# ACT's instructions in program order over 35 groups of a feed-forward stage

## The chip, the cores and the metric

The kernel runs on one core of a Trainium2 chip. The metric is the device time of one execution in microseconds (us), the median of three runs. A core has five engines that run beside each other, each through its own list of instructions in a fixed order: PE (TensorE, matmuls, with a separate weight load PEld), DVE (VectorE), ACT (ScalarE), POOL (GpSimd) and SP (SyncE, which here only issues DMAs). An instruction whose data are not ready holds up everything behind it on its engine.

## The reference

```python
x = x + 0.5 * ffn(layernorm(x), w1, b1, w2, b2)      # 256 -> 1024, relu, -> 256
u = layernorm(x)
K = 2 * real(einsum('hn,hnl->hl', Ct, exp(dtA * l)))  # 256 channels, N = 64 states
y = irfft(rfft(u, 2L) * rfft(K, 2L))[:, :L]           # causal convolution, L = 2048
x = x + (layernorm(u + y + u * D) * ln_w + ln_b)
x = x + 0.5 * ffn(layernorm(x), w1, b1, w2, b2)
```

x has the shape 8 x 2048 x 256 in float32. All matmuls with the weights are made in three parts (a high and a low half of each operand), so that they keep nearly full float32 accuracy.

## The kernel before

The tokens are worked on in 64 **groups** of 256. Stage a is the first feed-forward half step, stage b the second; between them the convolution is computed by chunks of 128 positions, with tables of powers of the states. This case is about stage a, and about the tables, which are built while it runs.

`sublayer` (L876) writes stage a out in **steps**, 8 to a group; step 3 of group 24 is called slot 24.3. One step takes one 128-wide chunk of the 1024 hidden columns:

- `up` (L851, matmul L857): 6 matmuls on PE into one of 4 PSUM banks `ph`.
- ACT: relu of that bank, the high half of the hidden tile `hx` (L946).
- DVE: max minus the high half, the low half of `hx` (L947, recorded at L116).
- `down` (matmul L867): 6 matmuls of the step that lies LAG = 3 steps behind, into `po`. So a relu must be done before the `down` three steps later.

Beside that each group has on ACT two norms `xn` and two norms `u` (L726), the copy `xh` of the transposed input (L799), one square root (L686) and two DMA issues (store of x1 L1030, load of `xa` L1012); on POOL one `add_bias` (L773), which waits for ACT's `xn`. PE turns the input by four transposes up to group 43 (`pt_a`, L790); from group 44 on DMAs do it (`DMA_A = 44`).

The **background** is a generator, `chain(matrices(), early())`. `fill()` (L902) lets it make a step whenever a virtual time, 1.32 for each step of the stage, has passed the sum of its paces. So a planes' batch is due each 9.1 units (10.3 from the 18th on), and its instructions are traced between those of the stage. `matrices()` builds a table P in 32 batches, here called planes 0 to 31. Each goes through three parts, one pass of the loop (L648) apart:

- `make(bt)` (L590): six products on POOL, L599, L601, L603, L605, L607 and L609, into a buffer `p_of(bt)`. There are four buffers in each half of the 32, so `make(bt)` can write only when the batch four before it has been stored. L609 is the last.
- `spread(bt)` (L612): two ACT copies (L618) of the low and high 16 bits into the tile `planes`, then one transposing DMA on SP's queue (L620) from `planes` to `turned`, and a DMA of the table itself (L625). There is one `planes` and one `turned`, so the copies of a batch wait until the DMA of the batch before has read them.
- `transpose(bt)` (L628): the back copies out of `turned`, one on DVE and one on ACT (both L635), and the store of the turned table (L637).

```python
yield
yield
for w in range(2):
    tc.keep_in_program_order(A_.copy(planes[:, w], pu[:, w]))
    yield
tc.keep_in_program_order(nc.sync.dma_start(
    out=turned..., in_=planes..., transpose=True))
```

In the trace both tiles are named `planes` (the DMA is planes<-planes), and P's buffers are parts of the large tile `u`. Beside the three parts, `lags()` adds small products on POOL (L535, L537, L541), matmuls `pk` on PE (L549) and four DMA issues on POOL (L569).

What sets the order: a scheduler takes the traced instructions and puts those of each engine into the order in which its own timeline finds them ready. Two things bind it: `keep_in_program_order`, which pins an instruction against the other pinned ones of its engine, and `tc.manual_schedule(engines=...)`, inside of which the named engines follow the traced order as it is. Before, the latter is used only for ACT and DVE in the steps ahead of t = 0 of a stage (L920 to L927, closed at t == 0). So in steady state ACT's relus and norms are free to move past the copies of `planes`, and the copies past them.

Of the kernel before, what the change touches and what calls it, by code (L numbers as in the profile page):

```python
# [43 lines left out]
def macaron_s4d_kernel(  # L44
# [35 lines left out]
    XL = 8  # L80
    LAGS_BEHIND = 3
    PIN = 1
    PINF = "a1", "a2"
    MB = 1
    PINT = 1
# [23 lines left out]
    def bank(tag, name):  # L109
        return ps.tile([P, 512], F32, name=name, tag=tag, bufs=BANKS[tag])  # L110

    def slot(tag, shape, name, dtype=F32):
        return work.tile(shape, dtype, name=name, tag=tag, bufs=BUFS[tag])

    def stt(o, a, s, b, op0, op1):
        return V.scalar_tensor_tensor(out=o, in0=a, scalar=s, in1=b, op0=op0, op1=op1)  # L116
# [554 lines left out]
    def stats(srcs, name, pin=False, mv=None):  # L671
        st = stat.tile([P, NTB, 6], F32, name=f"st_{name}", tag="st")
        mv = moments(NTB, name) if mv is None else mv
        for i, src in enumerate(srcs):
            ins = V.bn_stats(st[:, i, :], src)
            if pin:
                tc.keep_in_program_order(ins)
        for i in range(NTB):
            V.bn_aggr(mv[:, i, :], st[:, i, :])
        return mv  # L680
# [64 lines left out]
    def halves(xt):  # L745
        return [xt[:, i, :] for i in range(NTB)]

    def ffn_in(xt, name, on_act=NTB, by_dma=False, joint=None, into=None):
# [7 lines left out]
        else:  # L756
            mv = stats(halves(xt), f"f{name}", name in PINF)
            yield
# [92 lines left out]
    def up(wt, xT, ph, fc):  # L851
        xh, xl = xT
        fs = slice(fc * P, (fc + 1) * P)
        n = 0
        for dc in range(NDC):
            for wp, xp in ((1, xh), (0, xl), (0, xh)):
                nc.tensor.matmul(  # L857
                    ph, wt[wp][:, dc, fs], xp[dc] if type(xp) is list else xp[:, dc, :], start=(n == 0), stop=(n == 3 * NDC - 1)
                )
                n += 1  # L860

    def down(wt, hs, po, fc):
        hh, hl = hs
        for i in range(NTB):
            tsl = slice(i * P, (i + 1) * P)
            for n, (hp, wp) in enumerate(((hl, 0), (hh, 1), (hh, 0))):
                nc.tensor.matmul(  # L867
                    po[:, i, :],
                    hp[:, tsl],
                    wt[wp][:, fc, :],  # L870
                    start=(fc == 0 and i == 0 and n == 0),
                    stop=(fc == NFC - 1 and n == 2),
                    skip_group_check=True,
                )

    def sublayer(w1t, w2t, pre, post, lead, tag, first=(), background=(), due=(), at=(), wide=None):  # L876

        xT, po, running = {}, {}, {}
        background = iter(background)
        due = dict(due)
        at = dict(at)
        now = [0.0, 0.0]
        last = {}

        def step():  # L890
            while spawned:
                key, what = spawned.pop(0)
                running["later", key] = what
            for key in list(running):
                try:
                    next(running[key])
                except StopIteration as e:
                    del running[key]
                    if key[0] == "pre":
                        xT[key[1]] = e.value  # L900

        def fill(until=None):  # L902
            while until or now[1] <= now[0]:
                pace = next(background, "end")
                if isinstance(pace, str):
                    due.pop(pace, None)
                    if pace == "end":
                        now[1] = math.inf
                    if pace in (until, "end"):
                        return  # L910
                else:
                    now[1] += pace

        W0, W1 = (wide.first, wide.end) if wide else (NG, NG)
        starts_at = {}
        for g in range(NG):
            sooner = wide.sooner(g) if wide else 0
            starts_at.setdefault(g * SLOTS - lead - sooner, []).append(g)

        ordered = ExitStack()  # L920
        if first or tag == "b" and MB:
            ordered.enter_context(
                tc.manual_schedule(engines={mybir.EngineType.Activation, mybir.EngineType.DVE})
            )
        for t in range(-lead, NG * SLOTS + LAG + 1):
            if t == 0:
                ordered.close()  # L927
            g, k, f = t // SLOTS, t % SLOTS // 2, t % 2
            if W0 <= g < W1:
                g0, fc = g // 2 * 2, (t - g // 2 * 2 * SLOTS) // 2  # L930
                if f == 0:
                    hx = wide.hidden()
                    for i in range(2):
                        pend[g0 + i, fc] = [h[:, i * TOK : (i + 1) * TOK] for h in hx]
                    ph = bank("h", f"ph_{tag}{g0}_{fc}")
                    up(w1t, wide.input(g0), ph, fc)
                    last[A_] = A_.activation(hx[0], ph, AF.Relu)  # L937
                    last[V] = stt(hx[1], ph, 0.0, hx[0].bitcast(F32), ALU.max, ALU.subtract)
            elif t >= 0 and g < NG:
                fc = 2 * k + f  # L940
                hx = slot("hx", [P, 2, TOK], f"hx_{tag}{g}_{fc}", F32R)
                hh, hl = pend[g, fc] = hx[:, 0], hx[:, 1]
                ph = bank("h", f"ph_{tag}{g}_{fc}")[:, 0:TOK]
                up(w1t, xT[g], ph, fc)

                last[A_] = A_.activation(hh, ph, AF.Relu)  # L946
                last[V] = stt(hl, ph, 0.0, hh.bitcast(F32), ALU.max, ALU.subtract)  # L947
            tb = t - LAG
            tw = t - WLAG
            if W0 * SLOTS <= tw < W1 * SLOTS:  # L950
                g0 = tw // (2 * SLOTS) * 2
                fc, i = divmod(tw - g0 * SLOTS, 2)
                if fc == 0:
                    po[g0 + i] = wide.result(f"po_{tag}{g0 + i}").rearrange("p (i m) -> p i m", i=NTB)
                down(w2t, pend.pop((g0 + i, fc)), po[g0 + i], fc)
                if fc == NFC - 1:
                    running["post", g0 + i] = post(g0 + i, po.pop(g0 + i))
            if 0 <= tb < NG * SLOTS and not W0 * SLOTS <= tb < W1 * SLOTS:
                gb, fc = tb // SLOTS, tb % SLOTS
                if tb % SLOTS == 0:  # L960
                    po[gb] = bank("o", f"po_{tag}{gb}").rearrange("p (i m) -> p i m", i=NTB)
                down(w2t, pend.pop((gb, fc)), po[gb], fc)
                for mark in [m for m, d in due.items() if d == gb]:
                    fill(mark)
                if tb % SLOTS == SLOTS - 1:
                    running["post", gb] = post(gb, po.pop(gb))
            for n in starts_at.get(t, ()):
                running["pre", n] = pre(n)
            if t == -lead:
                running["first"] = iter(first)  # L970
            step()
            if t >= 0:
                now[0] += 1.32
                with ExitStack() as behind:
                    for ins in last.values():
                        behind.enter_context(tc.issue_after(ins.ins))
                    fill()
            if t in at:
                at[t]()
        while running:  # L980
            step()
        fill("end")
# [285 lines left out]
    def begin():  # L1268
        for _ in range(sizes[1] // PB):
            next(head)  # L1270

    sublayer(
        w1t, w2t, pre_a, post_a, 19, "a", load_weights(), chain(matrices(), early()),
        {"half": NG // 2, "tables": NG * 3 // 4},
# [123 lines left out]
    def pre_b(g):  # L1398
# [8 lines left out]
        uc = [uo[:, i // CQ, :, i % CQ] for i in range(P - 1 - i0, P - 1 - i0 - NTB, -1)]  # L1407
        mv = stats(uc, f"r{g}", PIN & 2)
        yield
# [9 lines left out]
        for i in range(NTB):  # L1419
            xb = xt[:, i, :].rearrange("p (b h) -> p b h", h=BCH)  # L1420
            ins = stt(xb, uc[i], rs[:, i : i + 1], xb, ALU.mult, ALU.add)
            if PIN & 1:
                tc.keep_in_program_order(ins)
# [4 lines left out]
    def post_b(g, po):  # L1428
# [7 lines left out]
        )  # L1436

    sublayer(
        [wb1[:, i] for i in range(2)], [wb2[:, i] for i in range(2)], pre_b, post_b, 17, "b",
        wide=wide,  # L1440
# [33 lines left out]
```

## Time and profile before

| | us |
|---|---|
| runs | 1746.32, 1751.17, 1751.95; median 1751.17 |
| profiled execution | 1747.17 |
| its span, first to last instruction | 1745.3 |
| mean granted clock of PE in it | 0.994 of full speed |
| groups 14 to 48 of stage a | 183.9 to 618.1 |
| one group in a calm part: groups up to 43, from 44 | 11.94, 11.52 |
| first and last copy of planes (L618) | 221.1, 575.0 |

The profile is of one execution; its times count from the first instruction. A row of a timeline has start, length, engine, line, operation, output<-inputs with shapes and, in brackets, the idle time of the engine just ahead and what ended it. Rows of one kind that follow each other are put together (x6). A row of waits has what waited, for what, and the total, the number and the longest in us. A row of windows has the stretch, its length, and the busy time and number of instructions of each engine in it.

### The profile page before, as it was taken

Reading aid. Unit: us, or ns where it says so; the run is one execution under the profiler, and the core shown is the slowest. Engines: PE = TensorE matmul, PEld = TensorE weight load, DVE = VectorE, ACT = ScalarE, POOL = GpSimd, SP = SyncE. Lnnn points to the kernel's source line nnn. Section 1 sums busy time; section 2 is a strip of 40 time slices with the busy share of each in tenths; the row PEclk is TensorE's granted clock in tenths of the full one; section 3 lists DMA queues with packets and bytes.
Section 4 is the critical chain, followed back from the end, with each engine's and each line's share of the span. In section 5 each row is a group of like instructions: output and inputs, shape, how many; then the busy total and the mean of one; then the engine's idle time right before and its main releaser. Section 6 shows DMA issues by size and latency. Waiting matters only on the chain.

```text
span 1745.3 us, 38327 instructions
## 1 busy us (share of the span) xinstructions
PE 1713.1 (98%) x14263; PEld 1638.1 (94%) x14263; DVE 1368.3 (78%) x4591; ACT 968.4 (55%) x2040; POOL 586.3 (34%) x550
## 2 busy tenths in 40 slices
PE   9999999999999999999999899999999999999998
PEld 7999999989999999999999799999999999999998
DVE  6998776677777767766999788889888788788754
ACT  4555477677778755544555445555455455445533
POOL 1117989886776105111000132231222222222200
PEclk9999999999999999999999989999999999999999
DMA  5111166577666532236888912332223323222211
GB/s 191 47 40 53 49 178 164 160 199 205 188 167 190 134 85 68 73 91 194 263 259 260 292 49 72 70 90 56 67 73 73 73 67 79 73 67 73 63 48 37
DMA packets 276849, 204.24 MB, mean 117 GB/s; under 512 B 162740, under 2 KB 235188, under 8 KB 276150
## 3 DMA queue, kind: packets, MB, share of 16 engines
q1 hardware_dynamic: 249232, 168.08, 36.2%
q10 hardware_dynamic: 26502, 32.52, 5.9%
q8 instruction: 112, 1.84, 0.4%
q0 software_dynamic: 928, 1.19, 0.3%
q14 instruction: 75, 0.61, 0.1%
HBM read 91.89 MB, written 71.57 MB: 94 GB/s over the span
## 4 chain that ended last, share of the span: by engine, by line
PE 80%; DVE 12%; DMA 4%; issue 1%; ACT 1%; SPq 0%; POOL 0%; ACTq 0%; DVEq 0%
PE po_b L867 21%; PE ph_b L857 20%; PE po_a L867 19%; PE ph_a L857 18%; DVE e L1160 2%; DMA planes<-planes 2%; DVE te L1161 2%; DVE xsB L1163 1%; DVE xsA L1163 1%; PE pt_a L790 1%; DVE xsA L1162 1%; DVE xsB L1162 1%; DMA xa<-in_L_attn_x_dram 1%; DMA wb<-w_dram 1%; PE pv L1130 1%
## 5 line engine op out<-in xcount | busy, mean ns | idle before, releaser
L867 PE MATMUL po_a<-wa,hx_a 128*128 128x256 f32 x3072 | 454.7, 285 | 6.8 <-DVE hx_a L116 6.6
L857 PE MATMUL ph_a<-xh_a,wa 128*128 128x256 f32 x2048 | 456.4, 287 | 1.2 <-ACT xh_a L799 0.7
L867 PEld LDWEIGHTS po_a<-wa,hx_a 128*128 128x128 f32 x3072 | 405.3, 192 | 9.5 <-DVE hx_a L116 8.0
L857 PEld LDWEIGHTS ph_a<-xh_a,wa 128*128 128x128 f32 x2048 | 355.3, 193 | 4.3 <-ACT wa L194 1.5
L946 ACT ACTIVATE hx_a<-ph_a 128x256 fp32r<-128x256 f32 x512 | 193.8, 388 | 229.5 <-PE ph_a L857 207.4
L116 DVE SCALAR_TENSOR_TENSOR hx_a<-ph_a,hx_a 128x256 fp32r<-128x256 f32 x512 | 209.0, 414 | 121.8 <-ACT hx_a L946 119.8
L867 PEld LDWEIGHTS po_b<-wb,hb 128*128 128x128 f32 x2208 | 288.1, 191 | 14.4
L867 PE MATMUL po_b<-wb,hb 128*128 128x256 f32 x2208 | 292.6, 282 | 0.0
L857 PE MATMUL ph_a<-xl_a,wa 128*128 128x256 f32 x1024 | 290.3, 285 | 0.0
L857 PE MATMUL ph_b<-xh_b,wb 128*128 128x256 f32 (+1 forms) x928 | 249.8, 327 | 0.7 <-ACT xh_b L799 0.7
L937 ACT ACTIVATE hb<-ph_b 128x512 fp32r<-128x512 f32 x184 | 109.2, 594 | 162.1 <-PE ph_b L857 161.2
L857 PEld LDWEIGHTS ph_a<-xl_a,wa 128*128 128x128 f32 x1024 | 197.4, 193 | 0.6 <-DVE xl_a L801 0.4
L116 DVE SCALAR_TENSOR_TENSOR hb<-ph_b,hb 128x512 fp32r<-128x512 f32 x184 | 124.9, 679 | 83.3 <-ACT hb L937 81.0
L773 POOL TENSOR_TENSOR xa<-xa,hb 128x512 f32<-128x512 f32 x64 | 85.1, 1330 | 286.9 <-ACT xn L726 245.9
L857 PEld LDWEIGHTS ph_b<-xh_b,wb 128*128 128x128 f32 x928 | 167.3, 193 | 12.8 <-ACT xh_b L799 1.1
L857 PE MATMUL ph_b<-xl_b,wb 128*128 128x256 f32 (+1 forms) x464 | 151.1, 327 | 0.0
L857 PE MATMUL ph_b<-even,wb 128*128 128x512 f32 x576 | 149.0, 393 | 0.0
L867 PE MATMUL po_b<-wb,hx_b 128*128 128x256 f32 x864 | 126.5, 285 | 3.9 <-DVE hx_b L116 3.9
L867 PEld LDWEIGHTS po_b<-wb,hx_b 128*128 128x128 f32 x864 | 114.2, 193 | 4.8 <-DVE hx_b L116 4.5
L857 PEld LDWEIGHTS ph_b<-even,wb 128*128 128x128 f32 x576 | 102.4, 189 | 16.9
L773 POOL TENSOR_TENSOR u<-u,hb 128x512 f32<-128x512 f32 x32 | 46.4, 1449 | 177.0 <-ACT xn L726 144.6
L946 ACT ACTIVATE hx_b<-ph_b 128x256 fp32r<-128x256 f32 x144 | 54.0, 381 | 73.0 <-PE ph_b L857 67.9
(292 smaller groups left out, 3028.4 us busy)
## 6 DMA issues: line engine op xcount, KB each, us to landing
o<-u SPq DMA_DIRECT2D x32, 512.0 KB, 4.0
pt<-u SPq DMA_DIRECT2D x32, 512.0 KB, 4.0
tz<-kpad SPq DMA_DIRECT2D x64, 256.0 KB, 4.5
x_dram<-xa ACTq DMA_DIRECT2D x62, 256.0 KB, 2.1
xa<-in_L_attn_x_dram ACTq DMA_DIRECT2D x61, 256.0 KB, 3.0
pt<-pt SPq DMA_DIRECT2D x60, 256.0 KB, 3.7
ot<-o SPq DMA_DIRECT2D x48, 256.0 KB, 4.1
u<-x_dram SPq DMA_DIRECT2D x32, 256.0 KB, 2.8
```

The source lines that it names most:

```text
L116: return V.scalar_tensor_tensor(out=o, in0=a, scalar=s, in1=b, op0=op0, op1=op1)
L773: return G_.tensor_add(xt, xt, hb2.unsqueeze(1).to_broadcast([P, NTB, H]))
L790: nc.tensor.transpose(pt[:, dc * TOK + i * P : dc * TOK + (i + 1) * P], xn[:, i, dc * P : (dc + 1) * P], ident,)
L857: nc.tensor.matmul(ph, wt[wp][:, dc, fs], xp[dc] if type(xp) is list else xp[:, dc, :], start=(n == 0), stop=(n == 3 * NDC - 1))
L867: nc.tensor.matmul(po[:, i, :], hp[:, tsl], wt[wp][:, fc, :], start=(fc == 0 and i == 0 and n == 0), stop=(fc == NFC - 1 and n == 2), skip ...
L937: last[A_] = A_.activation(hx[0], ph, AF.Relu)
L946: last[A_] = A_.activation(hh, ph, AF.Relu)
L1130: ins = nc.tensor.matmul(pv[ri][c * N : (c + 1) * N, l, j0 * B : j1 * B], pts[c][:, l, ri * N : (ri + 1) * N], some(j0, j1)[:, :, BCH * bt ...
L1160: E.tensor_mul(t1, xv[:, :, :, j, :], wr_b)
L1161: E.tensor_mul(t2, xv[:, ::-1, :, j, :], wi_b)
L1162: E.tensor_add(xv[:, :, :, j + 1, :], xv[:, :, :, j + 1, :], t1)
L1163: E.tensor_add(xv[:, :, :, j + 1, :], xv[:, :, :, j + 1, :], t2)
```

## The change

One constant, and a branch in the loop of `sublayer`: in stage a, at step 112 (group 14) a `manual_schedule` for ACT alone is opened, at step 392 (group 49) it is closed. What is traced for ACT in between stands on ACT in the order of the program. No instruction is added, removed or changed in shape. Since the scheduler follows the moved ACT instructions with the other engines, POOL's, DVE's and SP's orders differ in places too. Lines behind the first insertion are one higher after, lines behind the second nine.

```diff
@@ -80,6 +80,7 @@
     LAGS_BEHIND = 3
     PIN = 1
+    ACT_ORDER = 14 * 8, 49 * 8
     PINF = "a1", "a2"
@@ -925,6 +926,14 @@
         for t in range(-lead, NG * SLOTS + LAG + 1):
             if t == 0:
                 ordered.close()
+
+            if tag == "a" and t in ACT_ORDER:
+                if t == ACT_ORDER[0]:
+                    ordered.enter_context(
+                        tc.manual_schedule(engines={mybir.EngineType.Activation})
+                    )
+                else:
+                    ordered.close()
             g, k, f = t // SLOTS, t % SLOTS // 2, t % 2
```

## The prediction

> **What bounds it now.** First the page: where the span goes, and whether one engine fills it.
>
> ```profile
> span 1745.3 us, 38327 instructions
> PE 1713.1 (98%) x14263; PEld 1638.1 (94%) x14263; DVE 1368.3 (78%) x4591; ACT 968.4 (55%) x2040; POOL 586.3 (34%) x550
> ```
>
> PE (TensorE) is busy for 98%, so the change, which touches no matmul, can win only where PE stands still. Next, the stretches of stage a between the 14th and the 49th group (busy us and counts of PE, its weight load, DVE, ACT, POOL; granted clock; DMA share; GB/s):
>
> ```profile
> core 0: us, PE busy (x) PEld busy (x) DVE busy (x) ACT busy (x) POOL busy (x), PEclk, DMA share, GB/s
> ...
> 337.00:345.00 8.00, 6.15 (x39) 5.95 (x38) 5.76 (x18) 6.27 (x12) 1.33 (x1) 0.79 0.61 171
> 345.00:395.00 50.00, 45.86 (x379) 45.22 (x378) 34.86 (x130) 37.22 (x70) 42.52 (x39) 1.00 0.72 192
> ```
>
> PE lacks 1.85 us of 8 and 4.14 us of 50 here, and in the first stretch its clock is down. The stretches ahead and behind are full within 0.2 us each up to 545 us. What ACT waits for there (waits of ACT, 184 to 420 us), then the chain itself, ACT's and PE's timelines:
>
> ```profile
> ACT planes L618 <- DMA planes<-planes: 11.6, 9, 3.7
> ...
> ACT planes L618 <- POOL u L609: 1.3, 1, 1.3
> ```
> ```profile
> 332.09 0.38 ACT L946 ACTIVATE hx_a<-ph_a 128x256 fp32r<-128x256 f32 x1 [1.31 <-PE ph_a L857]
> 336.13 1.99 ACT L618 COPY planes<-u 128x1024 uint16<-128x1024 uint16 x2 [3.65 <-DMA planes<-planes]
> 338.03 1.32 ACT L635 COPY u<-planes 128x1024 uint16<-128x1024 uint16 x1
> 339.23 0.64 ACT L946 ACTIVATE hx_a<-ph_a 128x256 fp32r<-128x256 f32 x2
> ```
> ```profile
> 340.10 1.65 PE L867 MATMUL po_a<-wa,hx_a 128*128 128x256 f32 x6 [1.85 <-DVE hx_a L116]
> ```
> ```profile
> 392.93 0.98 PE L867 MATMUL po_a<-wa,hx_a 128*128 128x256 f32 x6 [2.86 <-DVE hx_a L116]
> ```
>
> Three copies stand back to back, with no relu between them. The first waits 3.65 us for the transposing DMA, and the next relu starts at 339.23, although its `up` matmuls ended at 333.94: 5.29 us late. `down` needs that relu, and PE stands. **Slack of a relu:** in a calm slot `down` starts 4.16 us after the end of `up`; relu start to end of DVE's second half takes 0.85 (slot 24.5: 317.39 to 318.24). So a relu may be 4.16 − 0.85 = 3.3 us late for nothing.
>
> **What PE loses between groups 14 and 49 before.** 0.97 in small gaps up to group 25, 1.85 at 338, 1.5 from half clock (the clock row 340.14 to 343.55; 16 matmuls at 0.21 instead of 0.12 us), 0.92 at 353.6, 0.36 at 356.9, 2.86 at 389.8, and 1.4 in small gaps: 9.9 us by group 33. That is all the change could give.
>
> **What the change moves.** By the instruction orders of both programs nothing is added or removed; planes 18 to 31 stand within one slot of where they stood, planes 0 to 17 do not. Written group.slot of the relu ahead: plane 6 copies from 22.5 to 21.6 and 21.7; plane 8 from 25.3 to 23.4 and 23.5; plane 9 from 25.6 to 24.3 and 24.4; plane 10 from 26.2 to 25.1 and 25.3; plane 12 from 28.5 to 26.7 and 27.0. From plane 6 on copies stand 7 slots apart, about 7 × 1.49 = 10.4 us. The back copies (L635, ACT and DVE) stand 6 to 10 slots after them, and SP's transposing DMAs and table stores follow.
>
> *Spreading.* Between two copies now stands at least one relu, except where the back copy follows the second. A bunch of 1.05 + 1.05 + 1.37 = 3.5 us shrinks to 1.05, or 2.4, under the 3.3 of slack. If the data were there, the 1.85, 0.92, 0.36 and 2.86 would go, with the 1.5 of clock: a gain of 7.5.
>
> *Coming early.* A copy can't start until POOL has made its plane (last product L609). Rows of POOL between planes 0 and 9:
>
> ```profile
> 218.80:329.30 110.50, 110.38 (x924) 109.65 (x922) 81.03 (x285) 78.09 (x147) 100.50 (x101) 1.00 0.59 166
> ```
> ```profile
> 328.01 1.29 POOL L609 TENSOR_TENSOR u<-u 128x512 f32<-128x512 f32 x1
> ```
> ```profile
> 314.07 0.38 ACT L946 ACTIVATE hx_a<-ph_a 128x256 fp32r<-128x256 f32 x1 [0.41 <-PE ph_a L857]
> ```
>
> Plane 9 is finished at 329.3; of the 110.5 us since plane 0, POOL was busy 100.5, so no order makes it much earlier: what stands ahead of it on POOL is the same set in both programs. Before, its copy came at 336.1 and the plane was ready. After, it comes behind relu 24.3, which ran at 314.07. ACT then stands, and every later relu, norm, xh copy, and both DMA issues of ACT's queue stand behind it. POOL's 10.0 us of idle were these:
>
> ```profile
> POOL u L599 <- DVE hx_a L116: 3.5, 1, 3.5
> POOL u L599 <- DVE mv_j L679: 2.0, 1, 2.0
> POOL xa L773 <- ACT xn L726: 1.4, 1, 1.4
> POOL u L541 <- PE pk L549: 0.9, 1, 0.9
> ```
>
> The 3.5 waits for a table's store to free the buffer; that store is no earlier after. 2.2 are gaps between dependent products. The other 4.3 may go or stay. Plane 9: 218.8 + 100.5 + 3.5 + 2.2 = 325.0 without them, 329.3 with all, 321.5 if the 3.5 went too. I take 327, the middle of the likely ends. Then copy 1.05, relu and DVE 0.85: 328.9. `down` of slot 24.4 started at 320.07, on an undisturbed grid (0.97 less) at 319.1. **PE slips 9.8 us** (4.3 at 321.5; 12.1 at 329.3). Plane 6 waits too: POOL, without the idle it can lose, ends it near 286.6, while ACT arrives near 280.4; that is 6.2 late, 2.7 of slip, and contained in the 9.8, since later waits shrink by what PE has slipped. The same holds for plane 8 (308.5 against 302.6).
>
> *Clock.* An idle start gap of 2.1 us before brought 3.4 us of half clock; 2.86 us at 390 brought none. A gap several times as long I price like the first, between 0 and 3.4; I take 2.0.
>
> The Trainium skill, "TensorE: Matmul & The Clock Gate", section "Part 1: The HAM clock gate (the "warmup" mystery)", says that the clock halves after an idle window of about 3.4 us and returns after as long a busy one. The 2.1 us row disagrees, the 2.86 us row agrees. By the page before should have lost nothing to the clock, and the one long gap after would cost about 1.7 us; so it speaks against the change, as the sum does.
>
> *After plane 9.* POOL's next chains are 5.0 us each: planes 10 and 11 near 332 and 337, ahead of their copies (25.1 is about 322 + 9.8 + 2 = 334). Plane 10's copies also wait for plane 9's transposing DMA: 0 to 2.4, I take 0.5. Later the loop copy, copy, DMA, next copy took 7.7 (336.1 to 343.8) to 9.1 us (343.8 to 352.9) before; with a relu between the copies about 0.5 more, 8.2 to 9.6 against 10.4: it fits, with little room. I take 1.0.
>
> **Sum.** After: 9.8 + 2.0 + 0.5 + 1.0 = 13.3. Before: 9.9. Net 3.4 us slower. The profiled execution took 1747.17 (span 1745.3 and 1.87 around it), so it would be 1750.6; the median of the three runs is 4.0 above that execution, and the same difference on it gives **1754.6**.
>
> **Rivals.** *Slower than can be missed, the loop of the planes:* the window from 345 to 420 us has the busiest DMA of the stage (share 0.72 and 0.79). If the transposing DMA then needs its longest, 7.5 us to landing instead of the median 4.7, the loop is 8.2 + 2.8 = 11.0 to 12.4, over 10.4, and each of planes 10 to 17 slips 0.6 to 2 us. It decides once the loop passes 10.4 us and the 3.3 us of slack are used up: 8 × 1.3 = 10, less 3.3, so 6.7 more: net +10, near 1761. For it: ACT already waited 11.6 us for that DMA. Against: behind plane 18 the same spaced order ran without loss.
>
> *Faster:* the 9.9 go and POOL's waits fit into the slack. That needs plane 9 by 313.1 + 3.3 + 1 = about 317 us; POOL would have to drop 100.5 to 98 us of work. Halfway (321.5, 4.3 lost, no clock drop) gives 9.9 − 4.3 = 5.6 less, near 1745.5; with all gone 1741. Against: POOL's 91% in that stretch.
>
> *It does nothing that matters:* the waits before were for the DMA, not for the order, and return at the same size: 1751.
>
> **Chances.** Forecast (one long wait at plane 9, then calm; net −2 to +7.5) 0.50; loop rival 0.36; faster rival 0.10; nothing 0.04. About 0.3%, 5.2 us, is what a measurement can tell from no change. Faster 0.10; within, 0.44 of the forecast and 0.04: 0.48; slower, 0.36 and 0.06: 0.42. Range 1745 to 1766: from POOL's early end (321.5) to its late one plus the loop (+2.3 + 6.7 + 2).
>
> **What would show it.** Right: PE idle by about 7 to 10 us in all between 285 and 330 us, behind a planes copy whose wait names POOL L609; the clock down right after; the idle at 338 and 390 gone; planes from 18 on unchanged. Loop rival: several waits of planes copies on DMA planes<-planes from 345 to 420 us, each with PE idle. Faster: no wait on L609 over 3.3 us. Wrong altogether: a loss behind 545 us, where no order differs.

## The result and the profile after

| | before | after |
|---|---|---|
| median, us | 1751.56 (1746.32 to 1753.08, 4 runs) | 1766.82 (1765.47 to 1767.19, 4 runs) |
| ratio, 95% interval | | 1.009 (1.0072 to 1.0109) |
| span of the profiled execution | 1745.3 | 1764.9 |

The change makes the kernel 15.3 us slower; 1754.6 was forecast, and the time lies 0.8 us above the range. The spans differ by 19.6, because the profiled execution of before was a fast one of its kind (1747.17 against the median). How it differs can be seen: four runs below keep before's places of the copies up to group 32 (program order from group 33 or 35 on), and at group 33 their traces are 2.6 to 3.3 us behind it, some 1.5 us of that by a stretch of half clock near 395 us.

The page of after, then the windows of after and those of before that the prediction does not show (columns as there):

```profile
span 1764.9 us, 38328 instructions
...
PE 1719.1 (97%) x14263; PEld 1640.1 (93%) x14263; DVE 1370.7 (78%) x4591; ACT 963.2 (55%) x2040; POOL 587.0 (33%) x550
```
```profile
250.00:300.00 50.00, 42.76 (x340) 41.69 (x339) 34.53 (x105) 30.50 (x58) 39.26 (x40) 0.97 0.54 150
300.00:337.00 37.00, 30.37 (x253) 30.17 (x253) 21.38 (x76) 21.97 (x42) 34.42 (x35) 0.95 0.66 171
337.00:345.00 8.00, 8.00 (x57) 8.00 (x58) 6.24 (x26) 5.37 (x12) 7.53 (x7) 0.82 0.85 245
345.00:395.00 50.00, 48.06 (x396) 47.04 (x395) 35.53 (x130) 35.72 (x69) 42.94 (x40) 1.00 0.67 189
420.00:545.00 125.00, 123.33 (x1014) 121.43 (x1013) 86.67 (x332) 87.82 (x172) 77.46 (x66) 1.00 0.57 165
545.00:635.00 90.00, 87.24 (x716) 85.91 (x715) 67.70 (x246) 64.91 (x131) 29.90 (x25) 1.00 0.53 144
```
```profile
250.00:300.00 50.00, 49.94 (x418) 49.56 (x418) 35.87 (x133) 35.55 (x68) 45.98 (x45) 1.00 0.66 180
300.00:337.00 37.00, 36.94 (x309) 36.59 (x308) 25.87 (x91) 22.67 (x45) 35.92 (x37) 1.00 0.50 147
420.00:545.00 125.00, 125.00 (x1050) 125.00 (x1049) 95.54 (x351) 94.26 (x181) 87.70 (x74) 1.00 0.63 177
545.00:620.00 75.00, 74.44 (x620) 74.27 (x620) 57.12 (x205) 57.09 (x114) 18.91 (x17) 1.00 0.57 146
```

PE is now idle 7.2 us between 250 and 300 and 6.6 between 300 and 337, where before had 0.06 each. It is less idle between 345 and 395 (1.9 instead of 4.1), and it lost 1.7 us between 420 and 545, where before had nothing, and 2.8 between 545 and 635, where before had 0.6 up to 620. To see when the lag arises I took the start of each group's first `down` matmul after, less the same before: 1.2 us in group 19, 2.4 at the start of 21, 11.0 in 22, 10.5 at 24.2, 18.2 at 24.6. Then before has its own stalls, and the lag falls: 14.6 in group 26, 12.9 at 33. From there it grows again, mostly by 0.4 to 0.5 a group and by 2.0 in group 42, to 20.4 at group 46. So there are **two losses**, one up to group 25 and one from 33 on. ACT's waits from 184 to 635 us name both:

```profile
ACT xn L727 <- DVE nb_u L120: 36.9, 22, 4.1
...
ACT planes L619 <- POOL u L610: 17.2, 4, 7.0
ACT planes L619 <- DMA planes<-planes: 16.5, 7, 4.3
```

In before, from 184 to 620 us, the same three rows are 8.1 us (9 waits, the longest 1.3), 1.3 (one wait) and 17.6 (16 waits, the longest 3.7). So the waits for DVE's constants and for POOL are new, those for the transposing DMA are not.

**The first loss.** Copies wait for POOL as forecast, but longer. The chain behind plane 6, from DVE's, SP's, POOL's and ACT's timelines of after (a queue's rows are DMA issues):

```profile
278.98 5.25 DVE L636 COPY u<-planes 128x1024 uint16<-128x1024 uint16 x1
```
```profile
284.29 1.93 SPq L621 DMA_TRANSPOSE planes<-planes  x1
286.27 0.99 SPq L638 DMA_DIRECT2D pt<-u  x1
```
```profile
291.21 1.06 POOL L600 TENSOR_TENSOR u<-u 128x512 f32<-128x512 f32 x1 [7.58 <-DMA pt<-u]
```
```profile
294.57 1.04 ACT L619 COPY planes<-u 128x1024 uint16<-128x1024 uint16 x1 [5.58 <-POOL u L610]
```

DVE's back copy of plane 4 takes 5.25 us. Plane 5's transposing DMA must wait for it, as it writes `turned`; the store of plane 4 stands behind that DMA on SP's queue. POOL's first product of plane 8 reuses plane 4's buffer and waits 7.58 us for the store. And plane 6's last product stands *behind* that first product on POOL. So the copy of plane 6, which ACT may no longer put off, waits 5.58 us, with the relus behind it. At plane 9 the same ring closes again: plane 7's store was issued at 325.10, POOL went on at 330.55 (2.03 us of idle, for which the view names no engine).

```profile
335.01 1.04 ACT L619 COPY planes<-u 128x1024 uint16<-128x1024 uint16 x1 [6.96 <-POOL u L610]
```

PE then shows both what the DVE copy did directly (it held up the low halves that stand behind it on DVE) and what plane 9 did:

```profile
285.64 1.65 PE L868 MATMUL po_a<-wa,hx_a 128*128 128x256 f32 x6 [4.42 <-DVE hx_a L117]
```
```profile
336.85 1.65 PE L868 MATMUL po_a<-wa,hx_a 128*128 128x256 f32 x6 [6.12 <-DVE hx_a L117]
```

The granted clock was at half from 285.3 to 288.7 and from 333.1 to 339.9 us.

**The second loss.** Slot 39.0 and 39.1 on ACT, before and then after:

```profile
499.55 0.38 ACT L946 ACTIVATE hx_a<-ph_a 128x256 fp32r<-128x256 f32 x1 [1.06 <-DVE nb_u L119]
499.90 1.09 ACT L726 ACTIVATE xn<-xa,nb_u,t_u 128x255 f32<-128x255 f32 x2
501.05 0.39 ACT L946 ACTIVATE hx_a<-ph_a 128x256 fp32r<-128x256 f32 x1
```
```profile
515.27 0.38 ACT L955 ACTIVATE hx_a<-ph_a 128x256 fp32r<-128x256 f32 x1 [1.12 <-PE ph_a L858]
516.99 1.09 ACT L727 ACTIVATE xn<-xa,nb_u,t_u 128x255 f32<-128x255 f32 x2 [1.33 <-DVE nb_u L120]
517.98 1.03 ACT L619 COPY planes<-u 128x1024 uint16<-128x1024 uint16 x1
518.92 0.37 ACT L955 ACTIVATE hx_a<-ph_a 128x256 fp32r<-128x256 f32 x1
```

The norm xn waits for DVE's constants `nb_u`, a copy stands behind it, and relu 39.1 comes 2.25 us after its matmuls instead of 0.10. Two slots on, relu 39.3 is 4.0 us late, over the 3.3 of slack, and PE loses 0.2 to 0.5 us. ACT's rows from `xh` to that relu, and PE's `down`:

```profile
521.46 0.59 ACT L800 CAST xh_a<-pt_a 128x512 fp32r<-128x512 f32 x1 [1.19 <-PE pt_a L791]
...
522.60 1.08 ACT L619 COPY planes<-u 128x1024 uint16<-128x1024 uint16 x1
...
523.56 0.39 ACT L955 ACTIVATE hx_a<-ph_a 128x256 fp32r<-128x256 f32 x1
```
```profile
524.47 0.98 PE L868 MATMUL po_a<-wa,hx_a 128*128 128x256 f32 x6 [0.18 <-DVE hx_a L117]
```

In DVE's order `nb_u` stands ahead of the low half of slot 39.0 in before, and behind it in after; the scheduler put the next group's statistics (`st_fa`) and that low half ahead of it:

```profile
499.07 0.58 DVE L119 TENSOR_SCALAR nb_u<-mv_j,t_u 128x1 f32<-128x1 f32 x4
499.57 0.42 DVE L675 BATCH_NORM_STATS2 st_fa<-xa 128x6 f32<-128x256 f32 x1
499.97 0.42 DVE L116 SCALAR_TENSOR_TENSOR hx_a<-ph_a,hx_a 128x256 fp32r<-128x256 f32 x1
```
```profile
516.20 0.41 DVE L117 SCALAR_TENSOR_TENSOR hx_a<-ph_a,hx_a 128x256 fp32r<-128x256 f32 x1
516.53 0.17 DVE L709 RECIPROCAL t_u<-q_u 128x4 f32<-128x4 f32 x1
516.74 0.58 DVE L120 TENSOR_SCALAR nb_u<-mv_j,t_u 128x1 f32<-128x1 f32 x4
```

### The profile page after: what moved, and what is told of

Same layout as the page of the kernel before. It is cut to its first block, busy times and chain, and to the rows that moved or that the text cites. A ratio compares the mean times of both kernels' runs of the same rounds, so it can differ in the third digit from the quotient of the medians.

```text
span 1764.9 us, 38328 instructions
## 1 busy us (share of the span) xinstructions
PE 1719.1 (97%) x14263; PEld 1640.1 (93%) x14263; DVE 1370.7 (78%) x4591; ACT 963.2 (55%) x2040; POOL 587.0 (33%) x550
## 4 chain that ended last, share of the span: by engine, by line
PE 72%; DMA 5%; DVE 4%; ACT 3%; issue 1%; POOL 0%; SPq 0%; ACTq 0%; DVEq 0%; POOLq 0%
PE po_b L868 20%; PE ph_b L858 20%; PE po_a L868 12%; PE ph_a L858 11%; PE py L1214 3%; PE pv L1139 3%; PE py L1205 2%; DMA pt<-pt 1%; DMA planes<-planes 1%; DMA xa<-in_L_attn_x_dram 1%; ACT u L727 1%; ACT planes L619 1%; DMA xb<-x_dram 1%; ACT hx_a L955 1%; DVE hx_a L117 0%
## 5 line engine op out<-in xcount | busy, mean ns | idle before, releaser
L858 PEld LDWEIGHTS ph_b<-xl_b,wb 128*128 128x128 f32 x464 | 89.8, 193 | 3.8
```

The costliest lines, as they stand in the source:

```text
L858: nc.tensor.matmul(ph, wt[wp][:, dc, fs], xp[dc] if type(xp) is list else xp[:, dc, :], start=(n == 0), stop=(n == 3 * NDC - 1))
```

## The experiments

Each run is told with its median and that of the kernel before on the same chip. All start from the changed kernel.

| run | us | before | ratio, 95% interval |
|---|---|---|---|
| e1 groups 33 to 48 only | 1762.72 | 1751.71 | 1.0062 (1.0048 to 1.0075) |
| e2 groups 14 to 32 only | 1762.19 | 1751.71 | 1.0054 (1.0040 to 1.0067) |
| e3 groups 25 to 32 only | 1754.86 | 1751.71 | 1.0026 (1.0015 to 1.0036) |
| e4 as e1, DVE too | 1764.42 | 1751.71 | 1.0067 (1.0055 to 1.0080) |
| e5 as e2, pace 10.3 | 1741.99 | 1750.26 | 0.9956 (0.9942 to 0.9970) |
| e6 before, pace 10.3 | 1740.07 | 1750.26 | 0.9944 (0.9925 to 0.9962) |
| e7 as e2, both back copies on ACT | 1778.84 | 1750.26 | 1.0154 (1.0132 to 1.0177) |
| e8 slot 27.4 to group 32 only | 1756.93 | 1750.26 | 1.0040 (1.0025 to 1.0055) |
| e9 groups 35 to 41 only | 1750.73 | 1751.01 | 1.0003 (0.9992 to 1.0014) |
| e10 as e9, DVE too | 1755.68 | 1751.01 | 1.0029 (1.0018 to 1.0039) |
| e11 after, pace 10.3 | 1746.86 | 1751.01 | 0.9980 (0.9969 to 0.9992) |
| e12 as e2, store ahead | 1764.83 | 1751.01 | 1.0082 (1.0066 to 1.0098) |

**e1 and e2: one part of the order at a time.**

```diff
-    ACT_ORDER = 14 * 8, 49 * 8
+    ACT_ORDER = 33 * 8, 49 * 8      # e1
+    ACT_ORDER = 14 * 8, 33 * 8      # e2
```

> ACT in program order only from group 33 to 48; up to there everything stands as before. The lag of the changed kernel's down matmuls grew by 7.5 us between groups 33 and 49, where the planes' copies stand almost where they stood. Theory 1 (two separate losses: up to group 33 the copies that wait for POOL, from 33 on norms xn that wait on ACT for DVE's constants nb_u with relus queued behind them): the late part alone costs 7 to 8 us, about 1759 us against 1751.5. Theory 2 (one loss; the late lag is only an after-effect of the early waits, since the background then runs at other places of the groups): as before, 1751 to 1752.

> ACT in program order only from group 14 to 32. Theory 1 (two separate losses): the lag reached by group 33 stays, 12.9 us, about 1764 us, and the waits of xn for nb_u behind 430 us are gone. Theory 2 (one loss with after-effects): all of the changed kernel's loss, about 1767 us.

Two losses, as theory 1 said, but the sizes only partly: the late part alone costs 11.0 us, the early part alone 10.5, and together 15.3. e2 loses little behind group 33 (its lag behind before's trace goes from 14.0 to 15.7). e1 pays 4.1 us in group 34, which the whole change doesn't: behind the place where the order is opened the copy of plane 20 waits 3.88 us for the transposing DMA of plane 19, and the clock halves at 453.5. Without that, e1's groups 36 to 40 take 12.3 to 12.7 us as in after, against 11.86 to 12.02 before.

**e3 and e8: the order opened behind the late planes.**

```diff
+    ACT_ORDER = 25 * 8, 33 * 8          # e3
+    ACT_ORDER = 27 * 8 + 4, 33 * 8      # e8
```

> ACT in program order only from group 25 to 32, so that planes 0 to 7 are copied where they were before, planes 8 and 9 in one bunch at slot 25.1, and planes 10 to 17 spaced as in the changed kernel. Theory 1 (the early loss comes from copies that ACT must make ahead of POOL's products; the spacing itself gains): no wait for POOL L610 over 3 us, the 7.5 us that before loses at 338, 354 and 390 us go, and the bunch at 25.1 costs 2 to 4: 1746 to 1749 us. Rival (program order is itself what costs, by the norms and the loop of the transposing DMA): no gain, 1751 to 1756 us.

> ACT in program order from slot 27.4 to group 32 only, behind the planes that POOL delivers late. Planes 0 to 11 stand as before, 13 to 17 are spaced. Theory 1 (spacing gains where the data are there): the 2.9 us of idle at 390 us and the half clock that some executions have behind it go: 1747 to 1749 us. Rival (opening the program order costs by itself, as the bunch at 25.1 did in the run from group 25): 1753 us or more.

Both were dearer than expected. PE, in the trace of e3 and then of e8:

```profile
340.29 1.65 PE L868 MATMUL po_a<-wa,hx_a 128*128 128x256 f32 x6 [9.98 <-DVE hx_a L117]
```
```profile
379.37 1.65 PE L868 MATMUL po_a<-wa,hx_a 128*128 128x256 f32 x6 [10.39 <-DVE hx_a L117]
```

Whatever was put off until then must be done where the order opens. In e3 ACT makes five copies and a back copy at slot 25.1, with no relu between, and waits 4.42 and 4.54 us for the transposing DMA; in e8 plane 12 is pinned at 27.6 and ACT waits for POOL (the last ACT row ahead of the idle, wait included):

```profile
371.16 1.99 ACT L619 COPY planes<-u 128x1024 uint16<-128x1024 uint16 x2 [7.18 <-POOL u L610]
```

Behind that both win, as the spacing should: e3's lag falls from 12.7 in group 25 to 7.3 by 33, e8's from 13.5 in group 29 to 10.4. So the spaced order does remove before's stalls, 3 to 5 us of them, and loses more where it meets a late plane.

**e5, e6 and e11: a slower pace, so that POOL is ahead of ACT.**

```diff
-        PA = 9.1
+        PA = 10.3                           # e5, e6, e11
+    ACT_ORDER = 14 * 8, 33 * 8              # e5
+    ACT_ORDER = 10000, 10001                # e6: never opened
```

> ACT in program order from group 14 to 32, and the background's pace slower there: 10.3 instead of 9.1 for a plane, so that plane 6 is copied at slot 22.5 instead of 21.6 and plane 9 at 25.4 instead of 24.3, about 13 us later. Theory 1 (the early loss of 10 us comes from copies that ACT must make before POOL has the plane, with the store of an older plane in the ring): POOL is in time, no wait for L610 over 3.3 us, PE loses at most 3 us up to group 33: 1745 to 1750 us. Rival (program order on ACT costs by itself: norms behind DVE, back copies, the transposing DMA): 1756 to 1762 us, as the run with the early part alone.

> The kernel before with the pace of 10.3 alone, no program order. The scheduler then spaces the copies by itself: but for plane 9 (26.0, 26.0) they stand within a slot of the run with program order at this pace. Theory 1: what bunched the copies of planes 8 to 13 before was POOL's lateness, not the missing order; the 7.5 us of stalls between 338 and 393 go: 1744 to 1748 us. Rival (the slower pace only moves the work: the last tables come two groups later, at 48 instead of 46, and something behind them waits): 1750 us or more, with the loss behind 600 us.

> The changed kernel whole (ACT in program order from group 14 to 48) at the pace of 10.3. If the late loss needs only DVE's late constants, it comes on top of the run with the early part at this pace (1742 us): 1748 to 1751 us. If it needs both, the late xn and a copy right behind it ahead of relu 1, it falls, since the copies stand at other slots of the group (39.1 and 39.3 instead of 39.0 and 39.2): 1742 to 1746 us.

So the first loss goes with the pace. At the slower pace the same program order costs nothing that counts (1741.99 against 1740.07 without it), and both are faster than before. It is not shown how much of it is POOL's: from e2 to e5, up to 420 us, ACT's waits for POOL's L610 fell from 17.4 to 8.8 us, but those for the transposing DMA from 15.6 to 1.8 as well, since the slower pace spaces the planes further apart. e6 also shows what the order was for: the scheduler spaces the copies by itself once the planes are there. Its PE between 337 and 395 us, and PE's waits from 184 to 640:

```profile
337.00:345.00 8.00, 8.00 (x70) 8.00 (x69) 5.86 (x27) 6.18 (x12) 7.32 (x7) 1.00 0.77 198
345.00:395.00 50.00, 50.00 (x422) 50.00 (x421) 36.93 (x137) 37.89 (x71) 45.51 (x41) 1.00 0.65 193
```
```profile
PE po_a L868 <- DVE hx_a L117: 0.4, 2, 0.2
```

6.6 us of waits in before are 0.4 here. **e6, one constant, has the lowest median of this study**: 10.2 us less than before. In the traces it leads before's by 8.6 us at group 63 and by 3.0 at the end; between them its execution had two stretches of half clock, at 810 and 977 us, that before's had not, which is at most 3.4 us of the 5.6. In e5 the copy of plane 9 still waits 7.37 us for POOL, though pinned a group later; e5's trace trails e6's by 6 to 7 us from group 26 on, its median by 1.9. The trace of e5 is of an execution of 1747.01 us, 5.0 above its median; in that of e11, whose PE, DVE, POOL and SP have the same order up to there, the same copy waits 3.37 us, and PE 0.7 in all up to 420 us instead of 4.5.

e11 adds the late part to e5: 4.9 us by the medians, 4.1 with each taken against its own before; between groups 32 and 46 its trace loses 6.1 us, that of e5 1.4. It lies under the 1748 to 1751 expected of a loss that needs only the late constants, and above the 1742 to 1746 of the other answer; the copies at 39.1 and 39.3 cost nothing in groups 38 and 39 (11.94 us), while other groups take 12.4 to 12.6 as in after. So both matter: the late xn, and where a copy stands behind it. The place that counts is a later one than I had named: in none of e11's groups 33 to 41 does a copy stand between xn and relu 1. In the seven that take 12.36 to 12.61 us one stands between `xh`, which waits for the transposes of the late xn, and relu 3; in groups 38 and 39 none does. In after the same separates groups 33 and 36 to 40 (12.41 to 12.67) from 34 and 41 (11.94); only group 35, at 12.39 without such a copy, does not fit. And e10 has such a copy in groups 36 to 40 with no wait of xn, and they take 11.94.

**e7 and e12: two links of the ring.**

```diff
-        P_REINT = (V.tensor_copy, A_.copy)
+        P_REINT = (A_.copy, A_.copy)                                          # e7
-            yield
-            nc.sync.dma_start(out=pt_dram[bt], in_=ptb)
+            tc.keep_in_program_order(nc.sync.dma_start(out=pt_dram[bt], in_=ptb))   # e12
```

> ACT in program order from group 14 to 32 at the old pace, and both back copies of a plane on ACT instead of one on DVE, so that no DVE copy can be held up beside POOL (5.25 us instead of 1.2 for plane 4 in the changed kernel). ACT has 1.37 us more for each plane. If that DVE copy starts the ring (DVE copy, transposing DMA, store, POOL's next make), the early loss halves: 1754 to 1758 us, and plane 6 is ready on POOL near 288 instead of 294.5. If POOL's amount of work sets it, as the prediction had it: no gain, 1762 us or more.

> ACT in program order from group 14 to 32 at the old pace, with the store of a turned table put ahead of the next plane's transposing DMA on SP's queue (in the changed kernel the store of plane 4 was issued at 286.27, after that DMA's issue of 1.93 us; POOL's next make waited 7.58 us for it). If the place on SP's queue is part of the ring: planes 6 and 9 are ready 2 to 4 us earlier on POOL than in the run with the early part alone (293.8, 334.5), and 1757 to 1760 us against 1762. If the DVE copy alone sets the ring, or SP puts the wait elsewhere: 1761 us or more.

In e7, without the DVE copy, POOL finishes plane 6 at 282.6 instead of 293.8 (e2), and plane 9 at 328.5 instead of 334.5. So that copy did start the ring: at the start of group 23 e7's trace is 3.3 us behind before's, e2's 10.3. The time didn't follow: group 24 costs it 7.9 us again, the lag at group 33 is 9.9 instead of 14.0, and 23 us more are lost behind it, where ACT carries both back copies in groups that have the scheduler's order. One row of ACT in e7 shows that plane 9 is still waited for:

```profile
328.56 1.04 ACT L619 COPY planes<-u 128x1024 uint16<-128x1024 uint16 x1 [7.41 <-POOL u L610]
```

In e12 the store of plane 4 is issued at 282.86, and planes 6 and 9 are ready at 290.4 and 330.1, 3.4 and 4.4 us earlier, as expected. The time was not better (1764.83). ACT's waits for the transposing DMA up to 420 us grew from 15.6 in e2 to 28.7: the shorter ring at POOL moved the wait to the next link. At group 33 its trace is 14.6 us behind before's, e2's 14.0; then it loses 5.8 more up to group 46, e2 1.7, as the edit holds for the later planes too.

**e4, e9 and e10: DVE's order in the late part.**

```diff
+    ACT_ORDER = 33 * 8, 49 * 8      # e4
+    ACT_ORDER = 35 * 8, 42 * 8      # e9, e10
-                        tc.manual_schedule(engines={mybir.EngineType.Activation})
+                        tc.manual_schedule(engines={mybir.EngineType.Activation, mybir.EngineType.DVE})   # e4, e10
```

> As the run with program order from group 33 to 48, but DVE follows the program there as well: its constants nb_u then stand behind the relu half of slot 6, ahead of the next group's statistics, some two slots ahead of the norm xn. If the late loss comes from DVE's constants, ordered late by the scheduler (theory 1), the waits of xn for nb_u fall under 0.5 us in all and the time is back at 1751 to 1753 us. Rival (the place of the copy between xn and relu 1, and the wait of xh for PE's transposes, cost it whatever DVE does): 1757 to 1760 us. A third way: DVE in program order waits for the transposing DMA with relu halves behind it, then over 1760 us and PE waits that end with DVE.

> ACT in program order from group 35 to 41 only, clear of the bunch that the order meets when it is opened at group 33. In the changed kernel these groups took 12.4 us instead of 11.94, each with xn waiting 1.3 us for DVE's nb_u. Theory 1 (DVE's order, which the scheduler makes later once ACT is fixed): the same 12.4 us for groups 36 to 40, 3 us in all, 1753 to 1756 us. Rival (the late loss is an after-effect of the early lag, or of where the planes stood): 11.94 us, no loss, 1750 to 1752 us.

> The same groups 35 to 41 with DVE in program order too: nb_u two slots earlier, the planes' copies where they stand in the run with ACT alone. If DVE's lateness costs the 0.45 us a group: 11.94 us for groups 36 to 40, xn waits under 1 us there, and 1750 to 1753 us, some 3 us less than ACT alone. If the copy between xn and the next relu costs it: 12.4 us again.

The mechanism holds, the times don't show it. With DVE in program order groups 36 to 40 take 11.94 us each in e10, and 11.94 to 12.10 in e4; with ACT alone, 12.31 to 12.67 in e1, and 12.5 in groups 39 and 40 of e9. In e9 the delay builds up slowly (groups 36 to 38 take 11.62 to 11.94, so three of the five expected at 12.4 were not), and its median can't be told from before. e4 and e10 lose more elsewhere, against before's trace: e4 3.6 us in group 34, as e1 does, 4.9 in group 42 and 1.7 and 1.8 in groups 44 and 45, e10 6.0 in groups 43 and 44, just behind the place where the order is closed. e4's median lies where the third answer put it (DVE held up by the transposing DMA), but DVE waited only 1.6 us for that DMA between 400 and 640 us. DVE in program order is therefore no remedy.

## Why the prediction was wrong, step by step

- *The wait at plane 9 names L610, PE stands behind it, the clock drops, the stalls at 338 and 390 go:* right in kind. The lag falls by 3.0 us in group 29, where before had its 2.9. The sizes were not: of PE's idle, forecast as 7 to 10 us between 285 and 330, only 3.1 lay there; 4.4 came just ahead, behind the DVE copy, and 6.1 just after.
- *Plane 9 at 327, between 321.5 and 329.3:* this step failed. It was 335.0. The term of POOL's work was right: 100.5 us from plane 0 on, and 99.82 busy of the 116.50 us from 218.5 to 335.0. The term of its idle time was 7.7 (327 less 218.8 and 100.5) and measured 16.7. I had written that the one store waited for "is no earlier after", and looked no further. It could be later, and there were three such waits (4.83, 7.58 and 2.03), because a late copy makes a late DMA, a late store and so a late product. (For the first the view names DVE's `xa`; it ended at 252.22, and the store of plane 1, issued at 248.31, landed at 252.06.) Before itself had two: the 2.0 that I left with what "may go or stay", put down to DVE's `mv_j` in its view, ended at 289.77, and plane 5's store, issued at 286.94, had landed at 289.55. The term failed first at plane 6, forecast near 286.6 and ready at 294.5. The idle ran in a ring through ACT, DVE, SP and POOL, and I had priced it as a list. A wait that an in-order engine passes on can return to it.
- *PE slips 9.8 us, and 2.0 for the clock:* with plane 9 at 335.0 instead of 327 the lag was 18.2 by slot 24.6 instead of 11.8. About 3.1 of it is the clock, estimated from the 6.2 us that PE worked at half of it (285.6 to 288.7 and 336.9 to 339.9). This is the first loss.
- *The DVE back copy:* in no term at all. Its row in before ran to 3.1 us against a median of 1.2, which was to be seen.
- *Nothing behind group 33:* this failed as well. I compared where the copies stand and found them within one slot; I did not compare DVE's order, nor ask what the norms on ACT wait for once nothing can pass them. That is the second loss, 7.5 us in the trace, and 4.9 by the medians of e5 and e11. Of the 7.5, 2.0 arise from group 43 on, which starts at 551 us in before: a loss behind 545 us, which I had named as the sign of being wrong altogether.
- *The loop of the transposing DMA, the slower rival:* in part. Copies of planes 12 and 13 waited 4.09 and 4.29 us for it at 364 and 377 us, but the lag grew by only 1 to 2 us there. It isn't what made the kernel slow. That rival's end and the forecast's were both under the measured time.
- *Coming early is the danger, spacing the gain:* right in kind; e5 and e6 show it.

Open: how the 15.3 us divide exactly, and how the first loss divides between POOL's lateness and the transposing DMA. The early and the late part alone give 10.5 and 11.0, which is more than the whole, since e1 pays for the place where its order opens.

## What to carry to other kernels

If an engine is put into program order, ask for each instruction that it may now wait for whether the producer is in time there, and follow that producer's own waits round until they end or come back to the first engine. Look at the order on all engines and not only at the instructions that one wanted to move: a scheduler that knows one engine is bound reorders the others. If a transfer between two engines comes too late, first try the rate at which the work is asked for: one constant gave 10 us here, while the order that was meant to repair the same stalls lost 15.

## What the runs showed of the hardware

- DVE's 16-bit copy of 128x1024 took 0.73 to 0.78 us while POOL was idle. It took 0.75 to 1.9 in most cases beside POOL's products, 2.30 once (before), and 3.12 (before), 4.58 and 5.25 us (after) where POOL's products followed one another with no gap between them. I didn't measure it by itself; e7, without that copy on DVE, had POOL's plane 6 ready 11 us earlier. The Trainium skill, "GPSIMD Engine Reference", section "1. Specifications", says that GpSimd shares its SBUF interfaces with VectorE, and names contention with DVE instructions in a 2-port mode or with two SBUF inputs. These rows agree with the sharing; whether this copy is of such a kind, and what ends its wait, no run here shows.
- Half clock came in stretches of 3.413 us or whole multiples (6.827, 10.24, 13.65 in e3). Idle of PE of 1.85 us was followed by one in before, idle of 1.98 (after, at 294 us) and 2.86 us (before, at 390) by none. The idle of 6.12 us in after brought two such lengths, partly inside the idle itself; the 10.39 of e8 three.
- What parts these cases is a grid. In each trace all stretches start on one grid of 3.413 us, so I summed PE's idle (ends as modelled) in every window of it. The 1.85 us of before lay in one window (336.72 to 340.14) and the next one was at half; the 1.98 was split 1.12 and 0.85, the 2.86 1.26 and 1.60. Over all 14 traces, from 30 to 1700 us, a full-clock window with 1.72 us of idle or more was followed by half clock, one with 1.71 or less was not, with one exception (1.87 in e1, at 1013 us). A window at half with up to 0.57 us of idle was followed by full clock, one with 0.62 or more by half again. So here about half a window of idle was enough, and a gap of 2 to 3 us cost about 1.7 us (half of 3.413) or nothing by its place in the grid.
- One constant order of instructions gave medians that repeat to about 1.5 us (before, 1750.26 to 1751.71), but single executions up to 9.4 us apart (1746.77 to 1756.16 in 29 of before), in part by these stretches.
